# Folding the norms of a two-layer graph attention network without TensorE's transposes, with new hand-written order lists

## The chip, the core and the metric

The kernel runs on one core of one Trainium2 chip, in one launch. The time is device microseconds of one execution; the time of a kernel is the median of its runs. The core's engines are PE (TensorE, matmuls and transposes; PEld are its weight loads), DVE (VectorE), ACT (ScalarE), POOL (GpSimd) and SP (SyncE, which here only issues DMAs).

## What is computed

The inputs are `x`, 64 graphs of 256 nodes with 512 features, and `adj`, 64 matrices of 256 x 256, all float32. Two layers follow each other (cut to what matters):

```python
# layer 0: attention with 8 heads of 64
q, k, v = x @ W_q + b_q, x @ W_k + b_k, x @ W_v + b_v
gate = k_nodes_of(x) @ w_g[512:]             # one bias for each attended node
y = x + softmax(q k^T / 8 + gate + log(adj + 1e-9)) @ v
# layer 1: two graph attentions, each behind a layer norm, with residuals
def gat(x, W, a_src, a_dst):                 # 8 heads, then 1 head
    h = x @ W
    s, t = sum(h * a_src, per head), sum(h * a_dst, per head)
    return softmax(leaky_relu(s_i + t_j, 0.2) + adj) @ h
z = y + gat(layer_norm(y, g1, b1), W1, a_src1, a_dst1)
out = z + gat(layer_norm(z, g2, b2), W2, a_src2, a_dst2)
```

## The kernel before

**A graph is a list of steps.** `graph(b)` is a generator, and each `yield` ends a named step. In order a graph has: "load", "turn" (X transposed by DVE in 32 x 32 blocks), "V", "V7", "V4", "Q", "Q7", "Q4", "K", "K7", "K4", two times "scores" (L569 matmuls of 64 rows, L576 exponentials on ACT), two times "mask" (L590: times the adjacency, two 128x1024 products on DVE; L595: one 128x1024 sum of the two halves, the "total"), "sums 0" (L378: softmax sums on PE from both totals; L385 reciprocal; the result goes through DRAM and comes back as rows R), "product 0" (L411 on PE), "gather 0" (L420 and L425 on DVE: times R, plus bias and residual; L293 to L296 on POOL), "tokens 1" (norm statistics on transposed features, L260 on PE, L275 to L277 on ACT), "V1", "V1 7", "V1 4", "rows 1" (attention ends through DRAM as rows; L653 products on DVE), eight "weights" (L665: two scalar_tensor_tensor of 128x256 on DVE each), "sums 1", "product 1", "gather 1", "tokens 2" (also L686 on POOL: adds the row of `b2 W2` to X2), "V2", "V2 7", "V2 4", "rows 2", "weights 2" (L716), and two times "product 2" (L728 on PE, then the output's DMAs).

**Projections.** Each of V, Q, K, V1 and V2 is a 2 x 2 block product with seven multiplications in place of eight (`winograd`, L317). The step with the bare name ("V") does five of them, "V7" the sixth, "V4" the seventh. A weight tile is `[128, 2, 7, 256 + more]`: four blocks of the matrix and three sums of blocks, which `combine` (L128) makes on DVE. `more` are extra columns behind each block: one for the gate in `wv`, one per head in `w1`, one in `w2`.

**The fold of the norms.** `fold_norm` changes W1 and W2 once, ahead of the first graph that needs them, so that the layer norm's scale, offset and mean cost nothing later. It (1) makes the extra columns, `W @ a_src` and `W @ a_dst` per head; (2) sums the rows of W weighted by `b` (the row `b W`, kept as row `bw`, as column `bwc` and, for the extra columns, as `off`) and by `g / 512` (the mean); (3) replaces W by `g W - mean`. It is also a generator, with steps "transpose", "columns" and "totals". Before the change it runs mainly on PE: 16 transposes of the blocks (L185) with ACT copies, 16 small matmuls with the spread vectors (L193), 16 matmuls of 128x264 (w1) or 128x257 (w2) with 128 equal weight columns (L213), and four transposes to turn `bw` into a column (L238); on DVE eight STT (L228) and `combine`. The spread vectors are filled by 18 POOL copies and memsets (L178), from columns that `load_columns` brought by DMA on ACT's queue.

**The order.** The instructions of PE are issued in the order of a list, written by hand: `start`, then a `period` that is repeated with the graph's number moved by one each time (the first number of a pair is the age of the graph; (0, "V") and (3, "V2") of one repeat belong to graphs b and b - 3), then `finish` (negative numbers count from behind the last graph). Before, `period` ends with

```python
(3, "V2"), (0, "scores"), (3, "V2 7"), (0, "scores"), (0, "mask"), (1, "rows 1"),
```

The other engines' orders come from the scheduler, which takes the list as the priority and looks at which tile buffers are free. PSUM tiles come from one ring of eight banks. The tag "ET" (four buffers of 128x2048) holds the exponentials of both attentions and the fold's transposes; the tag "X2" has four buffers of 128x512. W1 is loaded through SP's DMA queue when graph 1 begins, W2 when graph 2 begins, or at the fold's step "transpose" if that stands earlier.

After the last graph, 26 small operations on DVE (L363 to L365) and one transpose check that no value left its bounds. A second, plain version of the network stands behind them; its loop runs zero times here.

Of the kernel before, what the change touches and what calls it, by code (L numbers as in the profile page):

```python
# [9 lines left out]
F32 = mybir.dt.float32  # L10
# [10 lines left out]
def kernel(  # L21
# [127 lines left out]
    with ExitStack() as main:  # L149
# [6 lines left out]
        def ps(tag):  # L156

            return psum.tile([P, 512], F32, name=f"ps_{tag}", tag="ring", bufs=8)
# [4 lines left out]
        def fold_norm(name, w, g, b, sources, targets, heads):  # L163
# [6 lines left out]


            vectors = const.tile([P, KC, 2, heads], F32, name=f"vectors{name}")
            nc.gpsimd.memset(vectors, 0.0)
            for i, a in enumerate((sources, targets)):
                for h in range(heads):
                    lo, hi = (h % 2 * DH, h % 2 * DH + DH) if heads > 1 else (0, P)
                    chunk = slice(h // 2, h // 2 + 1) if heads > 1 else slice(0, KC)
                    nc.gpsimd.tensor_copy(vectors[lo:hi, chunk, i, h], a[lo:hi, chunk])  # L178
            yield
            wT = work.tile([P, KC, D], F32, name="wT", tag="ET", bufs=4)  # L180
            for m in range(KC):
                pt = ps("fold")
                for kc in range(KC):
                    block = w[:, kc % 2, BLOCKS[kc // 2, m // 2], m % 2 * P : m % 2 * P + P]
                    nc.tensor.transpose(pt[:, kc * P : (kc + 1) * P], block, ident)  # L185
                nc.scalar.copy(wT[:, m, :], pt)
            yield
            pt = ps("fold")
            more = w.shape[-1] - HD
            products = pt[:, : KC * 2 * heads].rearrange("p (k n) -> p k n", k=KC)  # L190
            for kc in range(KC):
                for m in range(KC):
                    nc.tensor.matmul(  # L193
                        products[:, kc, :], wT[:, m, kc * P : (kc + 1) * P],
                        vectors[:, m].rearrange("p i h -> p (i h)"),
                        start=(kc == m == 0), stop=(m == KC - 1), skip_group_check=True,
                    )
            for (k, n), at in BLOCKS.items():
                nc.vector.tensor_copy(
                    w[:, :, at, HD:], products[:, 2 * k : 2 * k + 2, n * more : (n + 1) * more]  # L200
                )
            yield
            columns, means = (
                data.tile([P, KC, P], F32, name=n, tag="X2", bufs=4) for n in ("columns", "means")
            )
            nc.scalar.copy(columns, b.unsqueeze(2).to_broadcast([P, KC, P]))
            nc.scalar.mul(means, g.unsqueeze(2).to_broadcast([P, KC, P]), 1.0 / D)
            got = {}
            for what, left in (("row", columns), ("mean", means)):
                for n in range(2):  # L210
                    pt = got[what, n] = ps(what)[:, : HD + more]
                    for kc in range(KC):
                        nc.tensor.matmul(  # L213
                            pt, left[:, kc, :], w[:, kc % 2, BLOCKS[kc // 2, n], :],
                            start=(kc == 0), stop=(kc == KC - 1),
                        )
            if name == "1":
                row = data.tile([P, D], F32, name="bw", tag="yS")
            else:
                row = const.tile([P, D], F32, name="bw")  # L220
            off = const.tile([P, 2, heads], F32, name=f"off{name}")
            for n in range(2):
                nc.scalar.copy(row[:, n * HD : (n + 1) * HD], got["row", n][:, :HD])
                nc.vector.tensor_copy(off[:, n, :], got["row", n][:, HD:])
            for kc in range(KC):
                for n in range(2):
                    block = w[:, kc % 2, BLOCKS[kc // 2, n], :]
                    nc.vector.scalar_tensor_tensor(  # L228
                        block, block, g[:, kc : kc + 1], got["mean", n], ALU.mult, ALU.subtract
                    )  # L230
            combine(w)
            stored = kept_rows.tile([1, D], F32, name=f"bw{name}")
            nc.sync.dma_start(out=stored, in_=row[:1, :])
            ordered = data.tile([P, KC, P], F32, name="ordered", tag="X2", bufs=4)
            nc.scalar.copy(ordered.rearrange("p k (a r) -> p k a r", a=4), by_chunk(row))
            pt = ps("fold")
            for m in range(KC):
                nc.tensor.transpose(pt[:, m * P : (m + 1) * P], ordered[:, m, :], ident)  # L238
            column = const.tile([P, KC], F32, name=f"bwc{name}")
            nc.vector.tensor_copy(column, pt.rearrange("p (m n) -> p m n", m=KC)[:, :, 0])  # L240
# [211 lines left out]
        def graph(b):  # L452
# [296 lines left out]
            (1, "mask"), (0, "V"), (2, "weights"), (4, "V2 4"), (0, "V7"), (3, "weights"),  # L749
            (1, "sums 0"), (1, "product 0"), (1, "gather 0"), (4, "rows 2"), (2, "weights"),  # L750
# [77 lines left out]
        with tc.manual_schedule(engines={mybir.EngineType.PE}):  # L828
# [24 lines left out]
            for key in ("w1", "w2"):  # L853
                next(graphs[key])
# [243 lines left out]
```

## Time and profile before

| | before |
|---|---|
| median of 3 runs | 3343.37 us (3339.86 to 3343.84) |
| the profiled execution | 3344.39 us |
| its span | 3342.6 us |
| PE busy | 3286.3 us (98%) |
| DVE busy | 2436.0 us (73%) |
| ACT busy | 1470.5 us (44%) |
| POOL busy | 935.9 us (28%) |
| DMA queue q1, share of 16 engines | 35.0% |

The span is the time from the first to the last record of the profiled execution; that execution took 1.8 us more. A "group" of the trace is a line, engine and operation with its tiles; "L317" is line 317 of the kernel before. Rows of the timeline give the start in us, the duration of the run of like instructions, the engine, line, operation, tiles, shape and number. A matmul's 128x257 tile in float32 is counted as four instructions where the row says x4 for two.

### The profile page before, as it was taken

How to read it: one execution, taken by the hardware profiler on the slowest of the kernel's cores; microseconds unless marked ns; L12 is line 12 of the kernel's file. 1: busy time of each engine (PE TensorE's matmuls, PEld its weight loads, DVE VectorE, ACT ScalarE, POOL GpSimd, SP SyncE). 2: the span in 40 equal slices, each digit the busy share in tenths (PEclk: the TensorE clock that was granted, in tenths of full speed). 3: DMA queues.
4: the chain of work that ended last, by engine and by line, in shares of the span. 5: the costliest groups of instructions: out<-in, count | busy, mean ns of one | idle time of the engine just before them, and what ended most of it. 6: DMA issues, size and time to landing. Idle time of an engine off the chain costs nothing. (4 is left out here: it accounts for less than half of the span.)

```text
span 3342.6 us, 80448 instructions
## 1 busy us (share of the span) xinstructions
PE 3286.3 (98%) x31146; PEld 2759.4 (83%) x31146; DVE 2436.0 (73%) x5277; ACT 1470.5 (44%) x4051; POOL 935.9 (28%) x1259
## 2 busy tenths in 40 slices
PE   7999999999999999999999999999999999999996
PEld 6888888888888888888888888888888888888875
DVE  4677777777777777777777777777777777777775
ACT  2444444444444444444444444444444444444442
POOL 1132232232232222322322322322322322322222
PEclk9999999999999999999999999999999999999998
DMA  4324334334334334333333333343333343343332
GB/s 107 101 81 115 100 97 112 103 91 116 105 89 118 104 90 116 101 95 112 99 102 110 95 108 104 93 115 101 96 112 103 91 115 105 88 118 103 90 102 57
DMA packets 270118, 339.42 MB, mean 102 GB/s; under 512 B 107918, under 2 KB 186786, under 8 KB 269732
## 3 DMA queue, kind: packets, MB, share of 16 engines
q1 hardware_dynamic: 268932, 333.67, 35.0%
q8 instruction: 249, 4.08, 0.5%
q14 instruction: 137, 1.12, 0.1%
q10 hardware_dynamic: 800, 0.55, 0.1%
HBM read 231.76 MB, written 102.31 MB: 100 GB/s over the span
## 5 line engine op out<-in xcount | busy, mean ns | idle before, releaser
L665 DVE SCALAR_TENSOR_TENSOR ET<-R,f,EA 128x256 f32<-128x256 f32 x1024 | 476.2, 531 | 145.7 <-PE ps_num L411 141.9
L411 PE MATMUL ps_num<-ET,V 128*32 128x256 f32 x8192 | 467.2, 380 | 0.0
L411 PEld LDWEIGHTS ps_num<-ET,V 128*32 128x32 f32 x8192 | 264.5, 110 | 155.0 <-issue 1.4
L590 DVE TENSOR_TENSOR ET<-ET,AT 128x1024 f32<-128x1024 f32 x256 | 311.1, 1232 | 95.2 <-ACT ET L576 95.2
L576 ACT ACTIVATE ET<-ps_sc,V 128x512 f32<-128x512 f32 x512 | 310.1, 690 | 121.9 <-PE ps_sc L569 121.8
L397 POOL TENSOR_TENSOR added<-added,inverse 128x128 f32<-128x128 f32 x128 | 69.7, 544 | 880.4 <-DVE inverse L385 788.3
L317 PE MATMUL ps_a<-w,S 128*128 128x264 f32 (+1 forms) x1024 | 273.6, 390 | 4.1 <-ACT m L614 4.1
L317 PE MATMUL ps_b<-w,S 128*128 128x264 f32 (+1 forms) x1024 | 266.5, 383 | 0.0
L293 POOL TENSOR_TENSOR S<-yT 128x256 f32<-128x256 f32 x64 | 77.6, 1212 | 660.2 <-PE ps_su L378 602.0
L569 PE MATMUL ps_sc<-QT,KT 64*128 64x256 f32 x2048 | 255.5, 389 | 0.0
L728 PE MATMUL ps_av<-V,ET 128*128 128x258 f32 (+1 forms) x1024 | 246.3, 384 | 9.0 <-DVE ET L716 9.0
L569 PEld LDWEIGHTS ps_sc<-QT,KT 64*128 64x128 f32 x2048 | 187.9, 187 | 58.1 <-issue 40.4
L317 PEld LDWEIGHTS ps_a<-w,S 128*128 128x128 f32 x1024 | 186.8, 189 | 54.9 <-ACT ET L576 19.5
L317 PEld LDWEIGHTS ps_b<-w,S 128*128 128x128 f32 x1024 | 193.9, 189 | 31.1
L728 PEld LDWEIGHTS ps_av<-V,ET 128*128 128x128 f32 x1024 | 186.9, 192 | 32.2 <-DVE ET L716 7.4
L686 POOL TENSOR_TENSOR X<-X,bw 128x512 f32<-128x512 f32 x128 | 159.8, 1270 | 165.8 <-ACT X L275 165.8
L653 DVE TENSOR_TENSOR V<-V,factors 128x256 f32<-128x256 f32 x256 | 195.9, 823 | 0.0
L420 DVE TENSOR_TENSOR ps_num<-ps_num,R 128x512 f32<-128x512 f32 x256 | 165.4, 690 | 27.6 <-DMA R<-kept 26.7
L277 ACT ACTIVATE ps_tr<-ps_tr,less 128x512 f32<-128x512 f32 x256 | 166.1, 649 | 0.1
L595 DVE TENSOR_TENSOR total<-ET 128x1024 f32<-128x1024 f32 x128 | 154.2, 1205 | 0.1
L317 PE MATMUL ps_a<-wv,xT 128*128 128x257 f32 x512 | 146.3, 408 | 6.4 <-DMA wv<-in_L_gnn_W_v_dram 3.0
L493 ACT ACTIVATE EA<-AT 128x512 f32<-128x512 f32 x64 | 40.3, 630 | 242.0 <-DVE ET L716 232.8
(176 smaller groups left out, 6917.2 us busy)
## 6 DMA issues: line engine op xcount, KB each, us to landing
R<-kept SPq DMA_DIRECT2D x128, 512.0 KB
X<-in_x_dram SPq DMA_DIRECT2D x256, 128.0 KB
kept<-xT SPq DMA_DIRECT2D x64, 512.0 KB
yT<-kept SPq DMA_DIRECT2D x64, 512.0 KB
R<-kept SPq DMA_DIRECT2D x512, 64.0 KB
kept<-yT SPq DMA_DIRECT2D x64, 512.0 KB
out_dram<-X SPq DMA_DIRECT2D x512, 64.0 KB
zT<-kept SPq DMA_DIRECT2D x63, 512.0 KB
```

Of the source, the lines that this page charges most:

```text
L277: nc.scalar.activation(pt, pt, AF.Square, bias=less[:, of], accum_out=squares[:, of])
L317: nc.tensor.matmul(to, A[:, kk, :], B[:, kk, :], start=(first and kk == 0), stop=(kk == 1), skip_group_check=not first,)
L411: nc.tensor.matmul(num[32 * a : 32 * a + 32, m * N : (m + 1) * N], V[:, j, a // 2, a % 2 * P + q * DH + 32 * m :][:, :32], pair[a // 2][:, ...
L420: nc.vector.tensor_tensor(both, both, R[:, q, :].unsqueeze(1).to_broadcast([P, 2, N]), ALU.mult)
L569: nc.tensor.matmul(banks[h % 2][:, o : o + N], KT[lo : lo + DH, (q + h) // 2, j * P : (j + 1) * P], QT[lo : lo + DH, (q + h) // 2, :], sta ...
L576: nc.scalar.activation(ET[:, j, i::2, :], banks[i].rearrange("p (h n) -> p h n", n=N), AF.Exp, bias=c[:, j, :],)
L590: nc.vector.tensor_tensor(ET[:, j, :, :], ET[:, j, :, :], AT[:, j, :].unsqueeze(1).to_broadcast([P, 4, N]), ALU.mult,)
L595: nc.vector.tensor_tensor(total, ET[:, 0], ET[:, 1], ALU.add)
L653: nc.vector.tensor_tensor(v, v, factors8[:, at : at + H // 2, :1].to_broadcast([P, H // 2, DH]), ALU.mult)
L665: nc.vector.scalar_tensor_tensor(ET[:, j, h, :], R[q][:, h, :], f[:, j, at : at + 1], EA[:, j, :], ALU.max, ALU.mult,)
L686: nc.gpsimd.tensor_tensor(X2[t], X2[t], folded["2"].row, ALU.add)
L728: nc.tensor.matmul(av[:, :width], ET[:, j, t * P : (t + 1) * P], V2[:, j, n, :width], start=(j == 0), stop=(j == NT - 1),)
```

## The change

It replaces the body of `fold_norm`, drops the four attention vectors from `load_columns`, and writes `period`, `start` and `finish` anew. In the file after the change, line numbers from the end of `fold_norm` on are 7 smaller (L317 is L310 there); this document keeps the numbers of before for unchanged lines.

In the new fold, `a_src` and `a_dst` come as rows, each broadcast to 128 partitions by a DMA on SP's queue. POOL multiplies the blocks of W by them (128x1024 each, four per fold), and DVE's tensor_reduce sums each product per head into the extra columns. `b` and `g / 512` are spread over 32 columns each (tile `left`), and 16 matmuls write four strips of 32 partitions of one bank: `b W` for both halves and the mean for both halves. ACT copies the bank, one row of each strip goes to DRAM, and DMAs bring the mean, `off`, the row and the column's chunks back; one small transpose makes the column.

```diff
             more = heads
-            (vectors filled by POOL; 16 transposes, ACT copies, 16 matmuls,
-             16 matmuls of full width for row and mean, 4 transposes)
+            for a in (sources, targets):
+                row = data.tile([P, D], F32, name="vector", tag="X2", bufs=4)
+                nc.sync.dma_start(out=row, in_=a.rearrange("h d -> (h d)").partition_broadcast(P))
+                vectors.append(row.rearrange("p (n f) -> p n f", n=2))
+            for kk in range(2):
+                blocks = w[:, kk, :4, :HD].rearrange("p (k n) f -> p k n f", n=2)
+                for i, row in enumerate(vectors):
+                    product = work.tile([P, 2, 2, HD], F32, name="product", tag="ET", bufs=4)
+                    nc.gpsimd.tensor_tensor(
+                        product, blocks, row.unsqueeze(1).to_broadcast([P, 2, 2, HD]), ALU.mult
+                    )
+                    by_head = product.rearrange("p k n f -> p k (n f)")
+                    nc.vector.tensor_reduce(
+                        w[:, kk, i:4:2, HD:], by_head.rearrange("p k (h d) -> p k h d", h=heads),
+                        AX.X, ALU.add,
+                    )
+            yield                                                  # "transpose"
+            left = data.tile([P, 2, KC, 32], F32, name="left", tag="X2", bufs=4)
+            nc.scalar.copy(left[:, 0], b.unsqueeze(2).to_broadcast([P, KC, 32]))
+            nc.scalar.mul(left[:, 1], g.unsqueeze(2).to_broadcast([P, KC, 32]), 1.0 / D)
             pt = ps("fold")
+            for kc in range(KC):
+                for i in range(4):
+                    nc.tensor.matmul(
+                        pt[32 * i : 32 * i + 32, : HD + more], left[:, i // 2, kc, :],
+                        w[:, kc % 2, BLOCKS[kc // 2, i % 2], :],
+                        start=(kc == 0), stop=(kc == KC - 1), skip_group_check=True,
+                    )
+            sums = data.tile([P, HD + H], F32, name="sums", tag="sums")[:, : HD + more]
+            nc.scalar.copy(sums, pt[:, : HD + more])
+            rows = sums.rearrange("(i r) f -> i r f", r=32)[:, 0, :]
+            kept = kept_rows.tile([4, HD + more], F32, name=f"sums{name}")
+            nc.sync.dma_start(out=kept, in_=rows)
+            (stored, mean, off, row and chunks by DMAs on SP's queue)
+            yield                                                  # "columns"
             (8 scalar_tensor_tensor w <- g w - mean, as before; combine(w))
             pt = ps("fold")
+            nc.tensor.transpose(pt[:, :KC], chunks, ident[:KC, :KC])
             column = const.tile([P, KC], F32, name=f"bwc{name}")
-            nc.vector.tensor_copy(column, pt.rearrange("p (m n) -> p m n", m=KC)[:, :, 0])
+            nc.vector.tensor_copy(column, pt[:, :KC])

 period = [
-    (1, "mask"), (0, "V"), (2, "weights"), (4, "V2 4"), (0, "V7"), (3, "weights"),
-    (1, "sums 0"), (1, "product 0"), (1, "gather 0"), (4, "rows 2"), (2, "weights"),
+    (2, "weights"), (1, "mask"), (0, "V"), (0, "V7"), (4, "V2 4"), (1, "sums 0"),
+    (1, "product 0"), (1, "gather 0"), (2, "weights"), (4, "rows 2"), (3, "weights"),
...
-    (1, "V1 4"), (0, "K4"), (3, "V2"), (0, "scores"), (3, "V2 7"), (0, "scores"),
-    (0, "mask"), (1, "rows 1"),
+    (4, "product 2"), (1, "V1 4"), (0, "K4"), (3, "V2"), (0, "scores"), (1, "rows 1"),
+    (0, "scores"), (3, "V2 7"), (0, "mask"),
 ]
 start = [
-    (0, "Q4"), (0, "K"), (0, "K7"), ("w1", "transpose"), (1, "load"), ("w1", "columns"),
-    (0, "K4"), (0, "scores"), (1, "turn"), (0, "scores"), (0, "mask"), (0, "mask"),
-    (1, "V"), ("w1", "totals"), (1, "V7"), (0, "sums 0"), (0, "product 0"), (1, "V4"),
...                                # w2: "transpose", "columns", "totals" among graph 0's layer 1
+    (0, "Q4"), (0, "K"), (0, "K7"), (0, "K4"), (1, "load"), (1, "turn"),
+    ("w1", "transpose"), ("w2", "transpose"), (0, "scores"), (1, "V"), ("w1", "columns"),
+    (0, "scores"), ("w1", "totals"), (0, "mask"), (0, "mask"), ("w2", "columns"), (1, "V7"),
+    (0, "sums 0"), (0, "product 0"), (1, "V4"), (0, "gather 0"), (2, "load"), (2, "turn"),
+    (1, "Q"), (1, "Q7"), (0, "tokens 1"), (1, "Q4"), (1, "K"), (1, "K7"), (1, "K4"),
+    (0, "V1"), (0, "V1 7"), (0, "V1 4"), (1, "scores"), (0, "rows 1"), ("w2", "totals"),
...
 finish = [
-    (-2, "product 1"), (-1, "weights"), (-1, "sums 1"), (-1, "product 1"), (-3, "rows 2"),
-    (-3, "weights 2"), (-2, "gather 1"), (-3, "product 2"), (-2, "tokens 2"),
-    (-3, "product 2"), (-2, "V2"), (-1, "gather 1"), (-1, "tokens 2"), (-2, "V2 7"),
-    (-1, "V2"), (-2, "V2 4"), (-2, "rows 2"), (-1, "V2 7"), (-1, "V2 4"), (-1, "rows 2"),
-    (-2, "weights 2"), (-2, "product 2"), (-2, "product 2"), (-1, "weights 2"),
-    (-1, "product 2"), (-1, "product 2"),
+    (-3, "weights 2"), (-1, "sums 1"), (-3, "product 2"), (-2, "tokens 2"),
+    (-1, "product 1"), (-3, "product 2"), (-1, "gather 1"), (-1, "tokens 2"), (-2, "V2"),
+    (-2, "V2 7"), (-2, "V2 4"), (-2, "rows 2"), (-1, "V2"), (-2, "weights 2"), (-1, "V2 7"),
+    (-1, "V2 4"), (-1, "rows 2"), (-1, "weights 2"), (-2, "product 2"), (-2, "product 2"),
+    (-1, "product 2"), (-1, "product 2"),
 ]
 ...
-            bq8, bv, gc1, bc1, gc2, bc2, *ac, wc = load_columns(      # 11 vectors
+            bq8, bv, gc1, bc1, gc2, bc2, wc = load_columns(           # 7 vectors
```

## The prediction

> **What bounds the kernel now.** I read the page first, then busy time by stretches, then PE's (TensorE's) instructions in order of time at the start, in the middle and at the end, then DVE (VectorE), POOL (GpSimd) and the DMA queue in the same stretches. The page, of the kernel before:
>
> ```profile
> span 3342.6 us, 80448 instructions
> ...
> PE 3286.3 (98%) x31146; PEld 2759.4 (83%) x31146; DVE 2436.0 (73%) x5277; ACT 1470.5 (44%) x4051; POOL 935.9 (28%) x1259
> ```
>
> PE lacks 56.3 us of the span. Stretches of 52.5 us show where (columns: PE, weight loads, DVE, ACT, POOL, granted clock, DMA share):
>
> ```profile
> 0.00:52.50 52.50, 35.20 (x191) 30.78 (x193) 16.40 (x34) 11.30 (x25) 9.24 (x48) 0.88 0.46 121
> 52.50:105.00 52.50, 48.33 (x384) 40.63 (x386) 30.36 (x54) 23.18 (x57) 12.78 (x14) 0.99 0.37 102
> ...
> 840.00:892.50 52.50, 52.50 (x495) 44.15 (x494) 39.43 (x87) 23.31 (x64) 14.52 (x19) 1.00 0.35 100
> ...
> 3255.00:3307.50 52.50, 44.94 (x399) 34.34 (x398) 33.72 (x87) 17.01 (x54) 21.04 (x28) 0.93 0.27 75
> ```
>
> From 210 to 3202 us PE never waits; 24.5 us of idle lie before that and 31.8 after. So the middle pays only for what PE executes, and the two ends for waits. PE's order in one period of the middle, then the same steps at the end, where the two score steps (L569) follow each other:
>
> ```profile
> 1006.81 1.03 PE L317 MATMUL ps_b<-w,S 128*128 128x257 f32 x4
> 1007.77 2.00 PE L569 MATMUL ps_sc<-QT,KT 64*128 64x256 f32 x16
> 1009.69 1.14 PE L317 MATMUL ps_a<-w,S 128*128 128x257 f32 x4
> 1010.76 2.00 PE L569 MATMUL ps_sc<-QT,KT 64*128 64x256 f32 x16
> 1012.68 1.14 PE L317 MATMUL ps_a<-wv,xT 128*128 128x257 f32 x4
> 1013.66 1.03 PE L317 MATMUL ps_b<-wv,S 128*128 128x257 f32 x4
> ```
> ```profile
> 3182.80 3.72 PE L569 MATMUL ps_sc<-QT,KT 64*128 64x256 f32 x32
> 3186.45 1.13 PE L317 MATMUL ps_a<-w,S 128*128 128x257 f32 x4
> 3187.43 1.03 PE L317 MATMUL ps_a<-wv,xT 128*128 128x257 f32 x4
> 3188.29 1.03 PE L317 MATMUL ps_b<-wv,S 128*128 128x257 f32 x4
> ```
>
> From the first score matmul to the second product of the next V it is 1013.66 - 1007.77 = 5.89 us when split and 3188.29 - 3182.80 = 5.49 together, for the same matmuls: 0.40 us for one more pair of turns between 128-row and 64-row matmuls. The fold of the norms on PE:
>
> ```profile
> 43.56 6.85 PE L193 MATMUL ps_fold<-vectors,wT 128*128 128x16 f32 x32
> ...
> 63.94 3.72 PE L213 MATMUL ps_row<-w,columns 128*128 128x264 f32 x16
> 67.50 3.72 PE L213 MATMUL ps_mean<-w,means 128*128 128x264 f32 x16
> ...
> 101.06 1.91 PE L185 MATMUL ps_fold<-ident,w 128*128 128x128 f32 x16
> ...
> 110.16 3.63 PE L193 MATMUL ps_fold<-vectors,wT 128*128 128x2 f32 x32
> ```
>
> **The change, part by part.** *Period.* The new list has scores, scores, "V2 7" in place of scores, "V2 7", scores, and V7 ahead of "V2 4". In the built program's order PE enters the score shape 125 times before and 69 after: 56 x 0.40 = 22.4 us off PE, in stretches where nothing else is on the path. The cover is thin. After two adjacent scores the six 128x1024 products and sums on DVE end 0.3 us ahead of "sums 0" (L378; first DVE's row, then PE's):
>
> ```profile
> 3192.20 1.18 DVE L595 TENSOR_TENSOR total<-ET 128x1024 f32<-128x1024 f32 x1
> ```
> ```profile
> 3193.59 1.08 PE L378 MATMUL ps_su<-total,ones 128*32 128x128 f32 x32
> ```
>
> The last total ends at 3193.30 (the next DVE row's start), PE needs it at 3193.59. The new period repeats just this order of DVE and ACT, and here PE did not wait, so I take the whole 22.4; bounds 0 and 24. V7 one product (0.87) earlier needs u2 from ACT, which lands 0.3 before it.
>
> *Fold, removed.* For w2, at full clock: L185 1.75, L193 3.49, L213 2 x 3.56, L238 0.45: 12.8 us. For w1 the same work took 6.95 + 6.69 + 7.12 + 0.44 = 21.2, of which 3.5 was waiting for W1, and the granted clock was 0.50 from about 40 to 53. A second drop at 114.9 cost 1.7 (sums and product 0 took 6.14 from start to start of the next, against 4.47).
>
> *Fold, added.* Per fold 16 matmuls of 32 columns in four strips; L411 runs 32 such of 256 columns in 3.57, so 1.8 each fold, plus one narrow transpose (0.1 to 0.3). But they wait for a chain, and PE's order is fixed. I walk it, with durations of rows of before:
> - SP now issues X and A of graph 1 (2.1 + 2.1) ahead of W1 (16 issues, 10.9 us): W1 32.4 to 43.3, then the store of xT (0.35), then the two broadcast rows (0.4 each). Such a row lands some 2.9 after its issue (the R loads at the end): 47.0. W2 with its rows follows, to 58.3.
> - POOL products of 128x1024. POOL took 0.73 for 128x256 and 1.27 for 128x512 (L686), so 2.36 by that slope. W1's four end at 56.5, W2's at 67.7. DVE's reductions are taken as L595 without contention, 1.18: the last ends at 57.8 and 69.0. Bound above: beside DVE's L590, POOL's L294 to L296 took 1.59 to 1.71 in place of 0.72; times 2.3, W2's last product comes 25 us later. Bound below: nothing, products cannot start before their rows.
> - PE: K4 37.3, scores, V of graph 1 to 44.6. Strips of w1 wait to 57.8 (13 us), second scores to 65, the small transpose waits for DMA (sums to DRAM, back as rows and chunks, about 2 us a hop) to 67, strips of w2 wait to 69.
> - Queued behind the reductions on DVE are the masks and totals of graph 0, the fold's eight L228 (3.47) and three of its L128: 69.0 + 6 x 1.22 + 3.5 + 0.8 + 2.0 = 82.6. "sums 0" waits for that (ran at 72.46), and "product 0" ends at 89.5, with 2.5 for half clock after idling, against 76.9: 12.6 later.
> - After this point before still pays w2's fold 12.8, the clock drop 1.7 and 4.5 of idle: 19.0. After pays about 8.3 of new waits: "tokens 1" now stands right behind Q7 (2.5, for R and four L425), the masks of graph 1 behind two products with R (2.9), and small ones (2.9).
> Start: 12.6 + 8.3 - 19.0 = +2 us. So the 25 us of PE work removed at full clock are paid back as waits. Bounds -10 and +14, wider above if POOL is slow. The four dropped vector DMAs (0.31 each on ACT's queue) and 18 POOL copies (3.9 us at 8.7) free nothing: V's first products wait for W_v through SP (13.01).
>
> SBUF contention weighs here: the L294 to L296 rows beside DVE. The Trainium skill's page "SBUF — State Buffer", section "Who interferes with whom", says that a DVE instruction with two SBUF inputs locks out a GpSimd read, and that tensor_reduce never does; in the built order only reductions stand on DVE beside these products. By that rule the 2.36 holds. By the L294 to L296 rows the start is +27 and the whole sum about zero.
>
> Half clock: the row is L193, 6.69 against 3.49, in a stretch at clock 0.50 lasting 13.6 us though PE was mostly busy. The Trainium skill's page "TensorE: Matmul & The Clock Gate", section "What's actually happening", has the rate halved after an idle window of about 3.4 us and restored after a busy one. That speaks against a change that makes PE wait 13, 4 and 9 us; by it each restart costs at most about 1.7, so 0.8 less than my 2.5 at "sums 0".
>
> *End list.* "V2" of the last graph now stands behind all of "V2" of the one before it, so the latter's row chain (7.7 us from its "V2 4" to L716 before) runs under seven products. The same walk from the last graph's scores gives 98 to 99 us to the last matmul, against 101.1 (3228.64 to 3329.7): more waiting ahead of "tokens 1" (4.6, was 2.2), less at the last two attentions. Ten of the 26 small checks on DVE (L363 to L365) move ahead of the last reciprocal, so the 5 us between the last X and the last transpose shorten by 2.5. End: -5; bounds -10 and +6.
>
> **Sum.** -22.4 + 2 - 5 = -25.4, on the profiled execution's 3344.39 (its span plus 1.8): 3319.0. That execution lies 1.0 above the median 3343.37, so 3318.
>
> **Rivals.**
> - *Totals late.* If the DVE chain after the scores grows by x, PE waits x - 0.29 in each of about 57 periods. At x = 0.69 the gain is gone, and from x = 0.85 the kernel is slower by over 0.2%. Two of the six operations beside POOL's factor sums (1.74 in place of 1.22) give 1.04: 0.75 x 57 = 43, hence 3361. For it: the slack is one quarter of one operation. Against: at 3185 to 3193 it held.
> - *Slow products.* POOL at the contended rate, +25: 3343, no change. For it: L293's 1.25 against 0.73. Against: DVE is otherwise idle there.
> - *Fold hidden.* The strips run nearly on time, because rows and products come earlier than I walk them: the start gains 25 instead of losing 2: 3291. For it: DMA is half idle. Against: eight products in series need 18.9 us after 47.
>
> **How the numbers follow.** Forecast 0.72, totals late 0.08, slow products 0.10, fold hidden 0.10. Start and end err apart from each other, and the period by 2: down sqrt(12² + 5² + 2²) = 13, up sqrt(12² + 11²) = 16, so 3305 to 3334; a little way into slow products and the hidden fold, 3302 to 3336. What a measurement here can tell from no change is about 0.2%, 6.7 us. Faster by more: the forecast, the hidden fold, and under half of the slow products: 0.86. Within: 0.06. Slower: totals late: 0.08.
>
> **What would show it.** Right: score blocks of 32 matmuls and a period of 50.18 us (from 50.58) with PE at 52.50 of 52.50 in the middle; PE waiting for DVE's reductions near 45 to 58 and for totals near 74 to 83; POOL products near 2.36. Wrong: a wait of L378 for the totals in every period, products over 4 us, or PE idle before 210 us under 20 us (I expect some 55).

## The result, and the profile after

| | before | after |
|---|---|---|
| median | 3343.75 us (5 runs, 3339.86 to 3343.84) | 3324.32 us (5 runs, 3322.89 to 3327.67) |
| the profiled execution, its span | 3344.39, 3342.6 us | 3324.74, 3322.9 us |
| PE busy, PE idle before 210 us | 3286.3, 24.5 us | 3246.7, 47.9 us |

The ratio is 0.9946, with a 95% interval of 0.9931 to 0.9960: 19.4 us less between the medians, 19.7 between the profiled spans. Forecast were 3318 us and a range of 3302 to 3336; the time lies in the range, 6 us from the forecast. In what follows every float32 matmul of the program counts as two in a row of the profile, and a kernel's rows carry its own line numbers (an experiment's differ from those of the kernel after by a few).

The page of the kernel after, and the same stretches as before (PE, weight loads, DVE, ACT, POOL, granted clock, DMA share and GB/s):

```profile
span 3322.9 us, 80192 instructions
...
PE 3246.7 (98%) x31044; PEld 2746.7 (83%) x31044; DVE 2443.8 (74%) x5273; ACT 1453.7 (44%) x4039; POOL 935.3 (28%) x1247
```
```profile
0.00:52.50 52.50, 30.46 (x177) 25.00 (x177) 18.67 (x35) 9.13 (x22) 11.36 (x33) 0.96 0.58 152
52.50:105.00 52.50, 35.00 (x297) 24.89 (x297) 34.98 (x57) 14.38 (x38) 18.84 (x14) 0.74 0.33 86
...
840.00:892.50 52.50, 52.50 (x498) 44.72 (x497) 39.87 (x88) 23.16 (x64) 14.57 (x20) 1.00 0.36 100
...
3255.00:3307.50 52.50, 40.66 (x373) 29.72 (x371) 27.47 (x75) 14.28 (x45) 13.01 (x17) 0.93 0.22 69
```

PE is full in the middle, as before, and does less there. The start has become emptier: of the second stretch PE fills 35.0 us, and 48.3 before, at a clock of 0.74 and 0.99.

To say where the 19.7 us lie, the span is cut at two points that both kernels have: the fifth "sums 0" counted from graph 0's as number zero, and number 58. Here and below the time of a "sums 0" is the start of its last matmul record. PE waits nowhere between the two points.

| stretch | before | after | difference | forecast |
|---|---|---|---|---|
| start to number 5 | 311.69 | 315.81 | +4.1 | +2 |
| number 5 to number 58 (53 periods) | 2680.56 | 2659.30 | -21.3 | -22.4 (56 periods) |
| number 58 to the end | 350.38 | 347.79 | -2.6 | -5 |

One period of the middle, the PE rows and then the DVE row that "sums 0" waits for:

```profile
1107.02 3.72 PE L562 MATMUL ps_sc<-QT,KT 64*128 64x256 f32 x32
...
1112.51 1.03 PE L310 MATMUL ps_b<-wv,S 128*128 128x257 f32 x4
...
1117.81 1.08 PE L371 MATMUL ps_su<-total,ones 128*32 128x128 f32 x32
```
```profile
1116.41 1.18 DVE L588 TENSOR_TENSOR total<-ET 128x1024 f32<-128x1024 f32 x1
1117.51 0.41 DVE L507 TENSOR_TENSOR V<-ps_c,m 128x257 f32<-128x257 f32 x1
```

From the first score to V's second product it is 1112.51 - 1107.02 = 5.49 us, the number that the end of the kernel before had shown, and the period is 50.18 us for 50.58. The last total ends no later than 1117.51, where DVE's next row starts, 0.30 us ahead of "sums 0". The start, PE first, then POOL's products (four of a fold in one row):

```profile
42.61 1.03 PE L310 MATMUL ps_b<-wv,S 128*128 128x257 f32 x4
56.74 2.01 PE L197 MATMUL ps_fold<-w,left 128*32 128x264 f32 x10 [13.10 <-ACT left L192]
59.97 2.86 PE L197 MATMUL ps_fold<-w,left 128*32 128x264 f32 x22 [1.22 <-DVE w L185]
...
82.52 1.71 PE L371 MATMUL ps_su<-total,ones 128*32 128x128 f32 x26 [6.32 <-DVE total L588]
...
164.55 1.95 PE L310 MATMUL ps_a<-wv,S 128*128 128x257 f32 x4 [3.92 <-ACT u L495]
```
```profile
49.41 9.25 POOL L181 TENSOR_TENSOR product<-w,vector 128x1024 f32<-128x1024 f32 x4 [8.46 <-DMA vector<-in_L_gnn_a_src_dram]
59.94 8.60 POOL L181 TENSOR_TENSOR product<-w,vector 128x1024 f32<-128x1024 f32 x4 [1.27 <-DVE w L185]
```

PE stands from 43.6 to 56.7 us, because the strips of w1 need the columns that POOL and DVE make, and again ahead of "sums 0", whose totals stand on DVE behind the eight reductions. The bracket at 56.74 names ACT's tile `left`; that copy itself waited for a buffer that a broadcast row held until POOL's third product, and the strips then wait 1.22 us more for the last reduction.

### The profile page after: what moved, and what is told of

The parts are those of the page before. It is cut to its first block, busy times and chain, and to the rows that moved or that the text cites. A ratio compares the mean times of both kernels' runs of the same rounds, so it can differ in the third digit from the quotient of the medians.

```text
span 3322.9 us, 80192 instructions
## 1 busy us (share of the span) xinstructions
PE 3246.7 (98%) x31044; PEld 2746.7 (83%) x31044; DVE 2443.8 (74%) x5273; ACT 1453.7 (44%) x4039; POOL 935.3 (28%) x1247
## 4 chain that ended last, share of the span: by engine, by line
PE 94%; DVE 2%; DMA 1%; SPq 1%; issue 1%; ACT 0%; POOL 0%; ACTq 0%; DVEq 0%; POOLq 0%
PE ps_a L310 20%; PE ps_a L317 14%; PE ps_num L404 13%; PE ps_b L310 10%; PE ps_b L317 7%; PE ps_sc L562 7%; PE ps_av L721 6%; PE ps_su L371 5%; PE ps_c L310 5%; PE ps_tr L253 4%; PE ps_c L317 3%; SPq L121 1%; DMA R<-kept 1%; DMA kept<-inverse 0%; DVE ET L583 0%
## 5 line engine op out<-in xcount | busy, mean ns | idle before, releaser
L658 DVE SCALAR_TENSOR_TENSOR ET<-R,f,EA 128x256 f32<-128x256 f32 x1024 | 463.2, 518 | 138.0 <-PE ps_num L404 136.9
L583 DVE TENSOR_TENSOR ET<-ET,AT 128x1024 f32<-128x1024 f32 x256 | 304.2, 1222 | 78.8 <-ACT ET L569 78.8
L569 ACT ACTIVATE ET<-ps_sc,V 128x512 f32<-128x512 f32 x512 | 303.1, 702 | 90.2 <-PE ps_sc L562 90.0
L310 PE MATMUL ps_a<-w,S 128*128 128x264 f32 (+1 forms) x1024 | 273.3, 389 | 1.1 <-ACT m L607 1.1
L310 PE MATMUL ps_b<-w,S 128*128 128x264 f32 (+1 forms) x1024 | 266.5, 383 | 0.0
L286 POOL TENSOR_TENSOR S<-yT 128x256 f32<-128x256 f32 x64 | 64.0, 1000 | 666.2 <-PE ps_su L371 595.5
L562 PE MATMUL ps_sc<-QT,KT 64*128 64x256 f32 x2048 | 241.2, 385 | 0.0
L310 PEld LDWEIGHTS ps_a<-w,S 128*128 128x128 f32 x1024 | 187.1, 189 | 51.4 <-issue 19.2
L310 PEld LDWEIGHTS ps_b<-w,S 128*128 128x128 f32 x1024 | 193.9, 189 | 31.0
L614 ACT ACTIVATE V<-ps_a,rstd 128x257 f32<-128x257 f32 (+1 forms) x128 | 61.2, 478 | 220.2 <-PE ps_a L310 220.2
```

The costliest lines, as they stand in the source:

```text
L310: nc.tensor.matmul(to, A[:, kk, :], B[:, kk, :], start=(first and kk == 0), stop=(kk == 1), skip_group_check=not first,)
L562: nc.tensor.matmul(banks[h % 2][:, o : o + N], KT[lo : lo + DH, (q + h) // 2, j * P : (j + 1) * P], QT[lo : lo + DH, (q + h) // 2, :], sta ...
L569: nc.scalar.activation(ET[:, j, i::2, :], banks[i].rearrange("p (h n) -> p h n", n=N), AF.Exp, bias=c[:, j, :],)
L583: nc.vector.tensor_tensor(ET[:, j, :, :], ET[:, j, :, :], AT[:, j, :].unsqueeze(1).to_broadcast([P, 4, N]), ALU.mult,)
L658: nc.vector.scalar_tensor_tensor(ET[:, j, h, :], R[q][:, h, :], f[:, j, at : at + 1], EA[:, j, :], ALU.max, ALU.mult,)
```

## The experiments

**1. The period of before with one pair exchanged.** Lists, fold, start and end of before.

```diff
-            (1, "V1 4"), (0, "K4"), (3, "V2"), (0, "scores"), (3, "V2 7"), (0, "scores"),
+            (1, "V1 4"), (0, "K4"), (3, "V2"), (0, "scores"), (0, "scores"), (3, "V2 7"),
             (0, "mask"), (1, "rows 1"),
```

> The kernel before, with one pair of the period exchanged: scores, scores, "V2 7" in place of scores, "V2 7", scores; fold, start and end as before. Theory (each separated score step costs one more pair of turns between 128-row and 64-row matmuls, 0.40 us): 57 more adjacent pairs, 57 x 0.40 = 22.8 us less, some 3321 us, a period of 50.18 us, no wait of PE in the middle. Rival A (the gain of the middle comes from the other moves of the new period, V7 ahead of "V2 4" and "rows 1" between the scores): no change, 3344 us, a period of 50.58. Rival B (totals late: with the scores adjacent the sums come too late for "sums 0" when "rows 1" still stands behind the mask): a wait of L378 for DVE's totals in each period, 3344 us or more.

Measured: 3319.13 us against 3342.51 for the kernel before, ratio 0.9928 (0.9912 to 0.9945): 23.4 us less, a period of 50.18 us, and no wait of PE in the middle. One exchange of two words gives as much as the whole change: its median is lower, but its interval overlaps that of the kernel after (0.9931 to 0.9960). Rivals A and B fall.

**2. The same pair exchanged back in the kernel after.**

```diff
             (0, "K4"), (3, "V2"), (0, "scores"), (1, "rows 1"),
-            (0, "scores"), (3, "V2 7"), (0, "mask"),
+            (3, "V2 7"), (0, "scores"), (0, "mask"),
```

> The kernel after, with one pair of the period exchanged back: scores, "rows 1", "V2 7", scores. Theory: 57 more pairs of turns, 22.8 us more, some 3347 us, a period of 50.58 us; the fold, the start and the end are as in the kernel after, so what is left against before is the +4 of the start and the -3 of the end. Rival A (other moves of the period carry the gain): 3324 us, a period of 50.18.

Measured: 3347.72 us, ratio 1.0017 to before (1.0007 to 1.0026), 23.4 us above the kernel after; a period of 50.57 us. PE's rows show the two halves apart again:

```profile
1115.45 2.00 PE L562 MATMUL ps_sc<-QT,KT 64*128 64x256 f32 x16
1117.38 1.13 PE L310 MATMUL ps_a<-w,S 128*128 128x257 f32 x4
1118.44 2.00 PE L562 MATMUL ps_sc<-QT,KT 64*128 64x256 f32 x16
```

Without adjacent scores the new fold and the new lists leave the kernel a little slower than before. The gain of the change is this one pair.

**3. Fold and start list of before, period and end list of after.** Against the kernel before:

```diff
         period = [
-            (1, "mask"), (0, "V"), (2, "weights"), (4, "V2 4"), (0, "V7"), (3, "weights"),
+            (2, "weights"), (1, "mask"), (0, "V"), (0, "V7"), (4, "V2 4"), (1, "sums 0"),
...
         finish = [
-            (-3, "scores"), (-3, "mask"), (-3, "mask"), (-2, "V"), (-4, "rows 1"), (-4, "weights"),
+            (-6, "V2 7"), (-3, "scores"), (-3, "mask"), (-4, "weights"), (-3, "mask"), (-2, "V"),
...
```

> The fold and the start list of before (PE does the fold), with the period and the end list of after. Theory (the new fold with its start list pays its PE time back as waits: fifth "sums 0" 4.1 us later than before): 4 us less than after, some 3320 us, with the fifth "sums 0" near 312 us from the start of the span. Rival C (the start loses by something else, such as the new period's first repeats or the granted clock): as after, 3324 us, fifth "sums 0" near 316.

Measured: 3318.58 us, ratio 0.9931 (0.9914 to 0.9947). The fifth "sums 0" comes at 311.16, against 311.69 before and 315.81 after. So the start's loss belongs to the fold and its list, and not to the period. Against experiment 1 (3319.13) the new end list is within the noise of the times; from number 58 to the end the two kernels with the old end list take 350.4 and 348.3 us, and ten with the new one (the kernel after, experiments 2 to 6 and 8 to 11) 345.0 to 349.2, 347.2 in the mean.

**4. The new fold in the start list of before.** Against the kernel after:

```diff
         start = [
...
-            (0, "Q4"), (0, "K"), (0, "K7"), (0, "K4"), (1, "load"), (1, "turn"),
+            (0, "Q4"), (0, "K"), (0, "K7"), ("w1", "transpose"), (1, "load"), ("w1", "columns"),
...
```

> The new fold (POOL, DVE, strips, DMAs) in the start list of before, with the period and the end list of after. Theory (the loss of the start is a matter of place: all eight POOL products in series ahead of the first totals): W1 is loaded ahead of graph 1's X here, and W2's fold stands behind graph 0's first layer. PE waits for W1's reductions at about 37 to 53 us instead of 44 to 57, "sums 0" of graph 0 comes near 75 instead of 82, W2's chain is covered: 5 to 10 us less than after, 3314 to 3320 us. Rival D (the chain rows, products, reductions, strips, DMA costs PE the same wait wherever it stands, once for each fold): W2's fold makes a second wait of 10 us or more near graph 0's second layer, 3325 to 3335 us.

Measured: 3326.96 us, ratio 0.9954 (0.9937 to 0.9970); the fifth "sums 0" at 319.37, 3.6 us later than in the kernel after. "sums 0" of graph 0 does come early, at 70.5 us (84.0 in the kernel after), but PE still stands ahead of w1's strips, and W2's fold brings waits of its own:

```profile
46.55 1.06 PE L197 MATMUL ps_fold<-w,left 128*32 128x264 f32 x2 [11.45 <-issue]
...
138.45 2.10 PE L253 MATMUL ps_tr<-ident,yT 128*128 128x128 f32 x8 [7.25 <-issue]
```

The first row is the wait for w1's reductions. Just ahead of the second, W2's small transpose waits 2.8 us for a DMA; then "tokens 1" of graph 1 waits 7.25 us, while DVE works through W2's eight L226 and two of its `combine` ahead of "gather 0". The theory was right on the first half and wrong on the second; rival D names the outcome.

**5. The fold put behind graph 0's first attention.** The start list alone is changed (and the rows are issued ahead of their W, as in experiment 6):

```diff
-            (0, "K4"), (1, "load"), (1, "turn"), ("w1", "transpose"), ("w2", "transpose"),
-            (0, "scores"), (1, "V"), ("w1", "columns"), (0, "scores"), ("w1", "totals"),
-            (0, "mask"), (0, "mask"), ("w2", "columns"), (1, "V7"), (0, "sums 0"),
+            (0, "K4"), (1, "load"), (1, "turn"), (0, "scores"), (0, "scores"), (0, "mask"),
+            (0, "mask"), (1, "V"), (1, "V7"), (0, "sums 0"), (0, "product 0"), (1, "V4"),
+            (0, "gather 0"), (1, "Q"), (1, "Q7"), (1, "Q4"), ("w1", "transpose"),
+            (0, "tokens 1"), ("w1", "columns"), ("w2", "transpose"),
```

> The kernel after, its start list changed alone: the fold's products, strips and spread stand behind graph 0's first attention and graph 1's Q and K, and the broadcast rows of the attention vectors are issued ahead of W1. Theory (the new fold costs the start nothing by itself; it costs because PE and DVE are made to wait for it ahead of work that is ready): "sums 0" of graph 0 at about 47 us (84 after, 73 before), V1 of graph 0 at about 73 (106 after), the fifth "sums 0" at 290 (316 after, 312 before): 3295 to 3305 us. Rival D (the chain costs the same wait wherever it stands): fifth "sums 0" at 310 to 320, 3320 us or more.

Measured: 3318.50 us, ratio 0.9931 (0.9914 to 0.9948). "sums 0" of graph 0 is at 51.3 us (47 expected), V1 of graph 0 only at 91.4 (73 expected), the fifth "sums 0" at 310.84 (290 expected). Of the 33 us gained at the first "sums 0", 15 were left at V1 and 5 at the fifth "sums 0". POOL's products began at 53.3, behind POOL's running sum of the inverses, and DVE's first two reductions for w2 stood ahead of seven of the eight L226 of w1 and of K's sums, so that PE waited 5.7 us for K; within V1 it waited 3.4 us for the end of w1's fold on DVE, and "tokens 1" of graph 1 waited 4.1. A miss of 20 us, and rival D's number.

**6. The rows issued ahead of their W.** One run. `fold_norm` gets a `yield` behind its two row DMAs, and is run up to it ahead of the load:

```diff
                     if (g, name) == (key, "transpose") or behind in graphs:
+                        next(graphs[key])
                         load_weight(nc.sync, t, w)
```

> The kernel after, with the two broadcast rows of each fold issued on SP's queue ahead of the 16 loads of its W instead of behind them; all else as it was. Theory (the chain starts when the last row lands, at 49.41 us): POOL's first product starts when W1 has landed, near 46.5, strips of w1 at 54 instead of 56.7, "sums 0" of graph 0 two to three us earlier, about 3322 us. Rival E (POOL is the limit only from W1's landing, which is as late as the rows): no change of the first product's start by more than 0.5 us.

Measured: one time of 3318.13 us, the first "sums 0" 2.3 us earlier (81.70 for 84.02), the fifth at 312.08 instead of 315.81. POOL's first product starts at 43.88 us (46.5 expected, 49.41 after). The rows were the last to land, as the theory had it, and in this run their place on SP's queue brings the fifth "sums 0" 3.7 us forward, nearly all that the start had lost. A single run does not settle it: experiment 2 has the start list of the kernel after too, and its fifth "sums 0" came at 318.28, 2.5 us later, of which two separated pairs of scores explain 0.8.

**7. The second total done twice.**

```diff
+                if tag == "KT":
+                    nc.vector.tensor_tensor(total, ET[:, 0], ET[:, 1], ALU.add)
                 nc.vector.tensor_tensor(total, ET[:, 0], ET[:, 1], ALU.add)
```

> The kernel after, with the second total of each graph (a 128x1024 sum on DVE) done twice: 1.2 us more on DVE ahead of every "sums 0". Theory of the prediction's first rival (slack of 0.3 us, so PE waits x - 0.3 in each period): 1.2 - 0.3 = 0.9 us in each of 57 periods, 51 us more, 3375 us, with waits of L371's line for DVE's total in every period. Against it (DVE makes the time good, or the scheduler moves other DVE work out of the way): no wait in the middle, 3324 us.

Measured: 3412.35 us, ratio 1.0212 (1.0192 to 1.0233), a period of 51.47 us. The waits of PE in the middle, and PE's rows of one period:

```profile
PE ps_su L371 <- DVE total L590: 52.0, 58, 0.9
```
```profile
1147.75 0.41 PE L371 MATMUL ps_su<-total,ones 128*32 128x128 f32 x4
1149.06 0.96 PE L371 MATMUL ps_su<-total,ones 128*32 128x128 f32 x26 [0.90 <-DVE total L590]
```

The wait is 0.90 us, 58 times, as the prediction's rival priced it: the slack is 0.3 us. But the period grows by 51.47 - 50.18 = 1.29, so a wait of 0.90 costs 0.39 more than itself. The rival's price per period was too low by that. Where 51 us more than in the kernel after were expected, the medians differ by 88; of the 87 between the profiled spans, 69 lie in the 53 periods and 9 each at the start and the end.

**8. Dummy matmuls in the two waits.** One run.

```diff
             pt = ps("fold")
+            if name == "1":
+                for _ in range(22):
+                    nc.tensor.matmul(pt[:, :HD], ident, wv[:, 0, 0, :HD], start=True, stop=True, ...)
```

> The kernel after, with dummy matmuls of 128x256 in PE's two long waits of the start: 22 ahead of w1's strips and 10 ahead of graph 0's "sums 0", into banks that are written anew behind them. If PE's half clock comes from idling: granted clock near 1 between 52 and 105 us (0.74 after), the second scores 2.0 us instead of 3.45, "sums 0" with "product 0" 4.5 instead of 6.2 after their wait, so that product 0 ends some 1.5 us earlier; the waits for reductions and totals keep their ends, and the whole is 3322 to 3324 us. If the clock follows something else (the DMA load or POOL's work), it stays at 0.74 and the dummies change nothing.

Measured: one time of 3328.70 us; the fifth "sums 0" at 319.58. The granted clock (before the DMA share) from 44 to 52 us, first of the kernel after, then of this one:

```profile
44.00:52.00 8.00, 0.00 (x0) 0.79 0.72 210
```
```profile
44.00:52.00 8.00, 8.00 (x39) 1.00 0.68 204
```

With PE kept busy the clock stays at 1.00 under nearly the same DMA load, so this drop follows PE's idling. Idling is not all that lowers it: in the kernel before, the clock was 0.50 from 114.9 to 118.3 us although PE stood nowhere between 99 and 136 us; L193's 32 records of 128x2 (110.16 to 113.65) stand ahead of that drop, and whether they caused it was not tried. The dummies did not help: PE still stood 4.5 us ahead of the strips, the clock fell again (0.50 from 55.8 to 66.1 and from 69.5 to 76.3 us), and a wait of 3.0 us before "tokens 1" brought a new drop at 96.8 us. Product 0 ended 0.7 us earlier, and 1.5 were expected.

**9 to 11. The chain freed of its queues.** Experiment 5 with both W loaded at once, graph 0's running sum on DVE, w1's products within graph 1's V and its strips within graph 1's Q, K ahead of "tokens 1":

```diff
-            unloaded = {"w1": (1, w1, W1), "w2": (2, w2, W2)}
+            unloaded = {"w1": (1, w1, W1), "w2": (1, w2, W2)}
-            nc.gpsimd.tensor_tensor(added, added, inverse, ALU.add)
+            (nc.gpsimd if begun else nc.vector).tensor_tensor(added, added, inverse, ALU.add)
+            begun.append(1)
-            (1, "V"), (1, "V7"), (0, "sums 0"), (0, "product 0"), (1, "V4"),
+            (1, "V"), ("w1", "transpose"), (1, "V7"), (0, "sums 0"), (0, "product 0"), (1, "V4"),
-            (0, "gather 0"), (1, "Q"), (1, "Q7"), (1, "Q4"), ("w1", "transpose"),
-            (0, "tokens 1"), ("w1", "columns"), ("w2", "transpose"),
+            (0, "gather 0"), (1, "Q"), ("w1", "columns"), (1, "Q7"), (1, "Q4"),
+            (1, "K"), (1, "K7"), (1, "K4"), (0, "tokens 1"), ("w1", "totals"), ("w2", "transpose"),
...
```

> The kernel after with the fold behind graph 0's first attention as in the run before, and four things in its way taken off: both W and their rows are loaded as soon as graph 1's inputs are issued; POOL's running sum of the inverses is done by DVE for the first graph alone, so that POOL's products do not queue behind that inverse; w1's strips stand within graph 1's Q; K of graph 1 stands ahead of "tokens 1" of graph 0. Theory (what holds the start up are queues in front of the chain, not the chain): POOL's first product near 46.5 us (53.3 in the run before), w1's strips by 62, V1 of graph 0 near 75 (91), the fifth "sums 0" between 290 and 300 (311): 3300 to 3310 us. Rival D (the chain itself sets the start): V1 near 90, the fifth "sums 0" near 310, 3318 us.

Measured: 3315.26 us, ratio 0.9915 (0.9898 to 0.9931), the lowest median of all; the fifth "sums 0" at 310.40 (290 to 300 expected). DVE's and POOL's rows say why it gave no more:

```profile
43.81 3.36 DVE L591 TENSOR_TENSOR total<-ET 128x1024 f32<-128x1024 f32 x1
47.09 3.35 DVE L586 TENSOR_TENSOR ET<-ET,AT 128x1024 f32<-128x1024 f32 x1
50.48 0.77 DVE L472 STREAM_TRANSPOSE AT<-A 128x256 f32<-128x256 f32 x2
51.17 1.18 DVE L591 TENSOR_TENSOR total<-ET 128x1024 f32<-128x1024 f32 x1
```
```profile
43.66 5.70 POOL L183 TENSOR_TENSOR product<-w,vector 128x1024 f32<-128x1024 f32 x2 [2.00 <-DMA w<-in_L_gnn_W_dram]
60.70 13.21 POOL L183 TENSOR_TENSOR product<-w,vector 128x1024 f32<-128x1024 f32 x6 [11.34 <-PE ps_num L407]
```

POOL starts at 43.7 as wanted, but its two products run beside DVE's sums and products of two inputs: these take 3.36 and 3.35 us in place of 1.2, POOL's 2.85 each in place of 2.31. Then POOL waits 11.3 us for a buffer of "ET", two of which graph 0 holds until "product 0". Two more kernels went after that, the first (which also puts w1's strips behind graph 1's "Q4") with

```diff
-                    product = work.tile([P, 2, 2, HD], F32, name="product", tag="ET", bufs=4)
+                    product = data.tile([P, 2, 2, HD], F32, name="product", tag="R", bufs=2)
```

> The run before, with two changes: POOL's products are written to the tag "R" (free until "rows 1") and not to "ET", of whose four buffers graph 0's exponentials hold two until "product 0"; w1's strips stand behind graph 1's "Q4". Theory (the third product waited from 49.4 to 60.7 us for a buffer of "ET"): the four products of w1 follow each other from 43.7, the last ends near 55, strips near 64; the DVE operations of graph 0's masks beside them take about 3.3 us in place of 1.2, so "sums 0" stays near 55. Fifth "sums 0" 303 to 309 (310.4 in the run before), 3308 to 3315 us. Rival (the buffer wait was hidden, R of graph 0 and the w2 reductions ahead of "gather 0" on DVE set V1): 3315 us.

Measured: 3318.50 us, ratio 0.9933 (0.9916 to 0.9950); the fifth "sums 0" at 307.74. The wait did not go: with two buffers of "R" the third product waits for DVE's first reductions, which stand on DVE behind graph 0's reciprocal, until 58.9.

The second, on top of it, with w2's load and its three steps moved behind graph 1's "gather 0", and w1's strips behind graph 1's "K":

```diff
-            unloaded = {"w1": (1, w1, W1), "w2": (1, w2, W2)}
+            unloaded = {"w1": (1, w1, W1), "w2": (B + 9, w2, W2)}
-            (1, "K4"), (0, "tokens 1"), ("w1", "totals"), ("w2", "transpose"), (2, "load"),
+            (1, "K4"), (0, "tokens 1"), (2, "load"),
...
-            (1, "sums 0"), (1, "product 0"), (1, "gather 0"), (0, "weights"), (2, "V4"), (2, "Q"),
+            (1, "sums 0"), (1, "product 0"), (1, "gather 0"), ("w2", "transpose"), (0, "weights"),
```

> As a_fold_own_tile, and w2's fold no longer beside graph 0's first layer: W2 is loaded and folded behind graph 1's "gather 0", where only PE is full; w1's strips stand behind graph 1's K. Theory (DVE's 11 us for w2 stood ahead of "gather 0" and of graph 0's V1): "tokens 1" of graph 0 near 70 us instead of 85, V1 near 78 instead of 92, and w2's products, reductions and spread hidden under PE: fifth "sums 0" 295 to 303, 3300 to 3308 us. Rival (DVE is as full there: w2's chain pushes masks and totals of graph 1 and 2, or waits for a buffer of "R" that graph 0's weights hold): fifth "sums 0" near 310, 3315 us or more.

Measured: 3320.05 us, ratio 0.9936 (0.9919 to 0.9952); the fifth "sums 0" at 312.60. V1 of graph 0 comes at 83.9, 8 us earlier than in experiment 9, and "tokens 1" of graph 1 then waits 8.9 us for "gather 0", two of w2's reductions and the weights of graph 0 standing ahead of it on DVE (the first reduction kept DVE idle for 2.1 us, until 116.1, waiting for POOL). The rival was right.

## Why the prediction was right, and where it was off

**The period: right, in cause and size.** 0.40 us for a pair of turns was read from two places of the kernel before; 53 periods gave 53 x 0.40 = 21.2 of the 21.3 measured, and experiments 1 and 2 show it alone, both ways. What they show is the price of a product between the two score blocks; that it comes from the turns between 64 and 128 rows, and not from the interruption as such, was not tried apart. The slack of 0.3 us that made "totals late" a rival is real (0.30 after, and 0.9 of wait for 1.2 of work in experiment 7), and it held. The cover was thinner than the rival had it: with the 0.39 of experiment 7 on top of each wait, a wait far shorter than the 0.40 of its break-even would have eaten the gain (an estimate from that one run).

**The fold's chain: right nearly to the microsecond.** The walk said: rows at 47.0 (49.4: they were issued 0.8 us later than walked, behind W1's 11.5 us of issues, and the rest is a longer way from issue to landing), a product 2.36 (2.31 for w1, 2.15 for w2), w1's last reduction 57.8 (59.9), the small transpose to 67 (69.8), the totals to 82.6 (82.5), product 0 ended at 89.5 (88.8). Of the nearest rows for POOL's price it had taken the L686 slope over the contended L294. The Trainium skill's page "SBUF — State Buffer", section "Who interferes with whom", which has a reduction never contend with GpSimd and a two-input DVE operation contend, agrees with the runs: POOL's 2.31 stands beside reductions of 1.22 after, and 2.85 beside 3.36 in experiment 9. The rival "slow products" is not borne out even there: beside two-input operations POOL's products took 2.85, and 3.14 at most (the first of w2 in experiment 11), where the rival's factor of 2.3 gives 5.4. It was DVE that paid the larger part.

**The rest of the start: the term that was too small.** From product 0's end to the fifth "sums 0" the kernel after wins 7.7 us back (234.76 before, 227.05 after), and the prediction had 19.0 - 8.3 = 10.7. The 19.0 stand (PE idle in this stretch before: 4.5, as said). The 8.3 of new waits was the term: "tokens 1" 2.1 to 2.3 (2.5 forecast) and graph 1's masks 2.3 (2.9), but "small ones" 2.9 were 5.9. Most of it is the row at 164.55: graph 3's sixth product of V waits 3.9 us for ACT's copy `u`, which stands on ACT behind the exponential of AT, which waits for DVE's transposes behind the masks:

```profile
161.55 1.21 DVE L583 TENSOR_TENSOR ET<-ET,AT 128x1024 f32<-128x1024 f32 x1
162.80 0.77 DVE L469 STREAM_TRANSPOSE AT<-A 128x256 f32<-128x256 f32 x2
163.60 0.63 ACT L486 ACTIVATE EA<-AT 128x512 f32<-128x512 f32 x1 [4.82 <-DVE AT L469]
164.14 0.36 ACT L495 COPY u<-ps_a 128x257 f32<-128x257 f32 x1
```

No such wait was in the walk, which at the start followed PE and DVE and not ACT's order; ACT's copy had been looked at for the period alone. The clock falls in it, so that "product 0" behind it starts 3.6 us after the wait's end and not 1.85, 1.7 more. Together that is 10.5 of waits for 8.3 and 1.7 of half clock, less some 0.9 that PE executes less: the 3.0 that are missing.

**The end: half of it.** -5 was 2.5 from the walk to the last matmul and 2.5 from the checks on DVE. The wait ahead of the last transpose did fall, from 5.2 to 2.5 us, and "tokens 1" of the last graph waits 4.9 (4.6 forecast). But from the last graph's first score to the last matmul's end it is 102.3 us and not 98 to 99 (101.1 before): the two waits before the last attentions came down by 0.7 us only, and after the second the last 16 matmul records took 5.42 us in place of 3.73, with the clock at 0.50 from 3308.4 to 3311.8. Other kernels with this end list spread over 4 us here, so a single profile cannot say more.

**"PE work is paid back as waits": shown.** PE is busy 19.3 us less up to the fifth "sums 0" (267.89 for 287.17) and idle 23.4 more. It expected some 55 us of idle before 210 us; 47.9 came.

Open is why no list brought the fifth "sums 0" below 307.7. Each experiment moved the wait: strips, "sums 0", K's sums on DVE, "tokens 1" of the next graph. The 3.9 us for `u`, the wait that the prediction had missed, stands in the kernel after and in experiments 2 and 5 to 10, and no experiment aimed at it; with the 1.7 behind it, it is more than the 4.1 that the start lost (an estimate, as other waits may grow in its place: experiment 11, without it, waits 5.3 us for totals there). The best new start (307.7) is 3.3 us ahead of the old fold's 311.0 of experiment 1. The kernels of 3315 to 3320 us (experiments 1, 3, 5, 9 to 11) overlap in their intervals, so an order among them is not shown. Their medians lie 4 to 9 us below the kernel after's, but no interval is clear of that of the kernel after; the lowest is experiment 9 with 3315.26 us, and the simplest experiment 1.

## What to carry to other kernels

Where one engine is full for nine tenths of the span, read what it executes in one period row by row: a pair of turns between matmul shapes that costs 0.4 us, saved some 57 times, was worth more than rebuilding a fold that had held 25 us of that engine's work. Work taken off the full engine at the start of a kernel gains only if nothing on the full engine's fixed order waits for the place where it went; walk the queues of all engines, ACT's too, since the one left out held the wait that was missed. Before a long POOL operation is put beside DVE, look at what stands on DVE then: here reductions cost nothing, and two-input operations slowed both, DVE most.

## What the runs showed of the hardware that was not expected

- A wait of PE costs more than itself. 0.90 us of wait lengthened the period by 1.29 (experiment 7); the 0.39 lies between the matmuls before and behind the stop. Some 0.24 of it can be the end of the last matmul before the stop, which the next one otherwise covers: a record of "sums 0" lasts 0.27 us, and without a stop the next starts 0.03 behind its start (an estimate, as a matmul's end is modelled). Whether it is the same cost as that of a turn between shapes, 0.40, was not tried. For the turn, the Trainium skill's page "TensorEngine Tiling (Array Packing)", section "Key Properties", says that a change of the tiling mode drains TensorE; the 0.40 us agree with it in sign.
- DVE pays for POOL: sums of 1.2 us took 3.36 beside one POOL product, while the product took 2.85 for 2.31.
- The granted clock is 1.00 or 0.50 in every trace here, and each stretch at 0.50, but for one that the end of a trace cuts, lasts a whole multiple of 3.41 us: in the kernel after 48.67 to 65.74, 69.15 to 75.98, 79.39 to 86.22 and 164.72 to 168.14. It fell 5.0, 2.9, 3.2 and 4.1 us after PE's last matmul (2.6 and 2.2 at two drops of experiment 8, the ends of matmuls being modelled), and came back 6.2, 3.7 and 3.6 us after a restart without a stop (from 69.81, 82.52 and 164.55). The Trainium skill's page "TensorE: Matmul & The Clock Gate", section "What's actually happening", has a free-running window of about 3.4 us; the multiples agree with it, and the drop 2.2 us after PE's last matmul shows that a window in which PE worked for a part can end in a drop. A wait of 3.9 us could thus cost 1.7 more, behind its end, and the restart at 69.81 some 3.1 (an estimate: half of 6.2), where the prediction had at most 1.7 for a restart.
